# A softplus series on GpSimd in place of VectorE, in the state space layer of a hybrid block

## The chip, the cores and the metric

The kernel runs on one core of a Trainium2 chip. A core has five engines that matter here, each with its own queue, which it works off in order: TensorE (PE, with its weight loads shown as PEld), VectorE (DVE), ScalarE (ACT), GpSimd (POOL) and SyncE (SP), which only issues transfers. The metric is the device time of one execution in microseconds, the median of three runs.

## The reference, cut to what matters

The block is four residual layers over 2 sequences of 1024 tokens with width 512: a state space layer, a mixture of experts, an attention layer, and the mixture again. Only the first one is touched. In it, all values float32:

```
xBCzA  = norm(x) @ in_proj.T                 # 2048 channels, 1024 gates z, 64 heads A_log
xBC    = silu(causal_conv4(xBCzA[:2048]) + bias)
dt     = softplus(A_log)                     # per token and head: 64 numbers a token
y      = chunked_scan(x, -dt, B, C, 128)     # decays are exp of sums of -dt in a chunk
y      = (y + D * x / dt) * silu(z + z_bias)
x     += y @ out_proj.T
```

The kernel makes softplus as max(a, 0) + log1p(exp(-|a|)), and the logarithm by a series: with y = exp(-|a|) and s = y / (y + 2), it is s times a polynomial of degree 8 in s squared, with the nine numbers of `ATANH`.

## The kernel before, in words

**Tiling.** A segment is 256 tokens, two chunks of 128, so there are 8 segments and 16 chunks. `segment_inputs` makes all that a segment needs. It is a generator: each `yield` is a step after which the caller may put in other work. Its first step makes the norm and the transposed tokens. Its second, which is called the head here, is the one that changes: `ps_dt` (L570) is A_log by 16 matmul records, `al` (L579) brings it to SBUF as a tile of 128x128 (128 tokens, two chunks of 64 heads), `sp_y` (L581) is -|a|, ScalarE takes its exponential in place (L582), and then come the instructions of the series: L584 (y + 2), L585 (reciprocal), L587 (s), L589 (s squared), L591 (first coefficient), L593 seven times, L594, and L596, which writes `dt`. After it come `dw` = D / dt (L599, L600). The third step has TensorE sum `dt` with three triangular or full matrices (`ps_cum`, L607), ScalarE takes the decays (`decay`, L609), VectorE copies the sums (`cum`, L612), and TensorE makes the same sums as rows (`ps_row`, L615), which go to DRAM (`sums`, L621) to be read back broadcast.

The 24 steps after it make the channels: `ps_ch` (L638) is 128 channels of the projection, in one of three buffers in PSUM that it shares with the gates' `ps_z` (L663). VectorE does the convolution, a first tap (L641) and three further ones (L645), and so frees the buffer; ScalarE takes the silu of four such tiles (L649).

**The chunks.** `own` takes one chunk: eight times it loads a tile `m` of 128x1024 (L802), GpSimd subtracts `cum` (L806), ScalarE makes two passes (L808, L809), VectorE multiplies by the masked scores (L810), and TensorE multiplies with x into `ps_y` (L814). VectorE multiplies by the gates (`yT`, L833) and TensorE projects out (`ps_out`, L840). `prologue` starts the next chunk: GpSimd makes `xd` and `y` (L718, L720), VectorE `yo` (L735), GpSimd adds it (L741) and scales the state (L764).

**Order.** The inputs of segment n+1 are traced beside the chunks of segment n: 27 steps over two chunks. The order of one engine's instructions isn't written out. The framework orders them once, when the kernel is built, by the order of tracing and its own estimate of when each operand is there, and sets the semaphores. On the chip each engine keeps to that order. So VectorE's queue holds series and convolution in turn, though the text emits the series in one piece.

**Buffers.** `al`, `sp_y`, `sp_r`, `sp_s2` have one buffer each, used once per segment. `dt`, `dw`, `decay` have two, `m` six.

Of the kernel before, what the change touches and what calls it, by code (L numbers as in the profile page):

```python
# [14 lines left out]
ALU = mybir.AluOpType  # L15
# [28 lines left out]
ATANH = [2.0 / (2 * k + 1) for k in range(9)]  # L44
# [45 lines left out]
def hybrid_layer_kernel(ctx: ExitStack, tc: tile.TileContext, a: dict, out: bass.AP):  # L90
    nc = tc.nc
# [426 lines left out]
    with ExitStack() as sa:  # L518
# [34 lines left out]
        def segment_inputs(b, s, before):  # L553
# [24 lines left out]
            al = sp.tile([P, n], F32, tag="al", name="al", bufs=1)  # L578
            nc.vector.tensor_copy(al, ps_dt.rearrange("p c h -> p (c h)"))  # L579
            y = sp.tile([P, n], F32, tag="sp_y", name="sp_y", bufs=1)  # L580
            nc.vector.scalar_tensor_tensor(y, al, -1.0, al, ALU.mult, ALU.min)  # L581
            nc.scalar.activation(y, y, AF.Exp)  # L582
            r = sp.tile([P, n], F32, tag="sp_r", name="sp_r", bufs=1)
            nc.vector.tensor_scalar(r, y, 2.0, None, ALU.add)  # L584
            nc.vector.reciprocal(r, r)  # L585
            sv = y
            nc.vector.tensor_mul(sv, y, r)  # L587
            s2 = sp.tile([P, n], F32, tag="sp_s2", name="sp_s2", bufs=1)
            nc.vector.tensor_mul(s2, sv, sv)  # L589
            acc = r  # L590
            nc.vector.tensor_scalar(acc, s2, ATANH[-1], None, ALU.mult)  # L591
            for c in ATANH[-2:0:-1]:
                nc.vector.scalar_tensor_tensor(acc, acc, c, s2, ALU.add, ALU.mult)  # L593
            nc.vector.scalar_tensor_tensor(acc, acc, ATANH[0], sv, ALU.add, ALU.mult)  # L594
            dt = sp.tile([P, CPS, NH], F32, tag="dt", name="dt")
            nc.vector.scalar_tensor_tensor(dt.rearrange("p c h -> p (c h)"), al, 0.0, acc, ALU.max, ALU.add)  # L596

            dw = sp.tile([P, CPS, NH], F32, tag="dw", name="dw")
            nc.vector.reciprocal(dw, dt)  # L599
# [258 lines left out]
        def inputs(n):  # L858
            b, s, _ = place_of(n * CPS)
            segs[n] = yield from segment_inputs(b, s, segs[n - 1][0] if s else None)  # L860
# [328 lines left out]
```

## Time and profile before

| what | value |
|---|---|
| runs | 2338.01 us median (2336.97 to 2341.95) |
| profiled execution | 2334.98 us, of which the span from first to last instruction is 2333.3 us |
| state space layer, 0 to 790 us of the span | PE 742.3 us busy, DVE 585.6, ACT 485.3, POOL 384.8 |
| the rest, 790 to 2333 us | PE 1488.8 us busy, DVE 828.9, ACT 371.0, POOL 655.5 |
| the eight heads begin (L579) at | 17.7, 73.3, 158.8, 255.8, 349.8, 439.4, 536.5, 636.7 us |
| L584 to L596 without L585, VectorE, all heads | 104 instructions, 46.3 us busy (4.7 + 4.9 + 7.4 + 6.2 + 18.7 + 2.2 + 2.2) |

A group's line gives line, engine, operation, tile written and tiles read, shapes, count, then busy time in us and the mean of one in ns, then the engine's idle time before it. A line of the timeline gives start and length in us, and in brackets how long the engine was idle before and what it waited for. A line of the waits gives the total in us, how often, and the longest.

### The profile page before, as it was taken

What the parts mean: (1) busy time and instruction counts of PE and PEld (TensorE: products, weight loads), DVE (VectorE), ACT (ScalarE), POOL (GpSimd) and SP (SyncE); (2) the same over time, 40 slices, a digit from 0 to 9 for tenths busy, and PEclk for the clock granted to TensorE, in tenths of its full rate; (3) what the DMA queues carried; (4) which work ended last, traced back from release to release, by engine and by line L of the source; (5) the groups of instructions that cost most, each with busy time, mean ns of one, the idle gap of its engine ahead of it and who ended that gap; (6) DMA issues with size and microseconds to landing.
All of it is one profiled execution on the core that took longest, in us unless ns stands there. A gap on an engine that the chain in (4) does not pass through costs nothing.

```text
span 2333.3 us, 29887 instructions
## 1 busy us (share of the span) xinstructions
PE 2231.1 (96%) x11018; PEld 1442.1 (62%) x11018; DVE 1414.5 (61%) x2115; ACT 856.3 (37%) x1414; POOL 1040.3 (45%) x695
## 2 busy tenths in 40 slices
PE   9999999999999999999789999999899999999998
PEld 7776677676776566555455656555566665565554
DVE  7777877777676630000339999884499999720002
ACT  4656576666566422221122332222223332212221
POOL 3544464455645300001457777642678776210002
PEclk9999999999999999999899999999999999999999
DMA  8444454454554477876355564433466554368766
GB/s 282 148 145 146 162 183 155 138 196 138 178 174 178 161 264 260 301 261 239 111 189 182 178 224 171 149 117 129 177 222 215 200 206 138 122 239 298 294 244 196
DMA packets 116369, 449.67 MB, mean 193 GB/s; under 512 B 15104, under 2 KB 17920, under 8 KB 103808
## 3 DMA queue, kind: packets, MB, share of 16 engines
q1 hardware_dynamic: 88960, 380.28, 46.9%
q0 software_dynamic: 12480, 40.90, 5.7%
q10 hardware_dynamic: 14784, 26.58, 3.0%
q8 instruction: 88, 1.44, 0.2%
q14 instruction: 57, 0.47, 0.1%
HBM read 402.09 MB, written 45.61 MB: 192 GB/s over the span
## 4 chain that ended last, share of the span: by engine, by line
PE 64%; DVE 13%; POOL 8%; DMA 6%; ACT 5%; issue 5%; SPq 0%; POOLq 0%; ACTq 0%; DVEq 0%
PE ps_o L476 13%; PE ps_g L445 12%; PE ps_u L454 11%; PE ps_ch L638 5%; PE ps_out L840 5%; POOL pr L1007 3%; PE ps_z L663 3%; DMA m<-sums 3%; DVE sc L1011 3%; PE ps_xnT L187 2%; PE ps_y L814 2%; DVE pv L1027 2%; DVE o L1028 2%; POOL m L806 2%; PE ps_hT L466 2%
## 5 line engine op out<-in xcount | busy, mean ns | idle before, releaser
L1007 POOL TENSOR_TENSOR pr<-qk 128x1536 f32<-128x1536 f32 x128 | 441.4, 3458 | 145.3 <-DVE sc L1011 71.0
L806 POOL TENSOR_TENSOR m<-m,cum 128x1024 f32<-128x1024 f32 x128 | 243.5, 1911 | 318.3 <-DMA m<-sums 221.5
L455 DVE TENSOR_TENSOR h<-h,ps_u 128x352 f32<-128x352 f32 x156 | 80.4, 515 | 479.8 <-PE ps_u L454 473.9
L380 POOL DMA_INDIRECT xg<-normed,r_tok x92 | 90.1, 979 | 539.3 <-PE ps_xnT L187 465.4
L638 PE MATMUL ps_ch<-xnT,w_ch 128*128 128x259 f32 x1024 | 260.1, 400 | 17.4 <-DVE chan L645 14.5
L476 PE MATMUL ps_o<-w_d,hT 128*128 128x512 f32 x552 | 254.5, 596 | 6.9 <-issue 3.7
L447 ACT ACTIVATE h<-ps_g 128x352 f32<-128x352 f32 x156 | 72.4, 464 | 494.7 <-PE ps_g L445 485.5
L1011 DVE TENSOR_REDUCE sc<-pr 128x32 f32<-128x1536 f32 x128 | 224.2, 1752 | 38.3 <-POOL pr L1007 38.2
L445 PE MATMUL ps_g<-w_gu,xT 128*128 128x352 f32 x736 | 237.0, 462 | 2.6 <-ACT hT L468 1.2
L454 PE MATMUL ps_u<-w_gu,xT 128*128 128x352 f32 x736 | 236.7, 461 | 0.0
L638 PEld LDWEIGHTS ps_ch<-xnT,w_ch 128*128 128x128 f32 x1024 | 192.6, 195 | 65.6 <-issue 34.4
L808 ACT ACTIVATE m<-m 128x1024 f32<-128x1024 f32 x128 | 134.4, 1053 | 184.9 <-POOL m L806 184.8
L476 PE MATMUL ps_o<-s_d,hT 128*128 128x512 f32 (+1 forms) x384 | 183.7, 611 | 12.6 <-ACT hT L468 10.3
L445 PEld LDWEIGHTS ps_g<-w_gu,xT 128*128 128x128 f32 x736 | 137.0, 190 | 91.0 <-issue 32.2
L482 ACT COPY y<-ps_o 128x512 f32<-128x512 f32 x92 | 53.9, 586 | 372.3 <-PE ps_o L476 372.2
L645 DVE SCALAR_TENSOR_TENSOR chan<-ps_ch,convw,chan 128x256 f32<-128x256 f32 x384 | 180.9, 476 | 7.4
L476 PEld LDWEIGHTS ps_o<-w_d,hT 128*128 128x128 f32 x552 | 104.9, 192 | 114.9 <-issue 92.3
L454 PEld LDWEIGHTS ps_u<-w_gu,xT 128*128 128x128 f32 x736 | 133.5, 191 | 63.0 <-issue 7.1
L445 PE MATMUL ps_g<-s_gu,xT 128*128 128x352 f32 x512 | 170.7, 469 | 1.4 <-ACT h L447 1.4
L454 PE MATMUL ps_u<-s_gu,xT 128*128 128x352 f32 x512 | 168.0, 466 | 0.0
L810 DVE TENSOR_TENSOR m<-m,g 128x1024 f32<-128x1024 f32 x128 | 150.6, 1211 | 20.0 <-ACT m L809 19.8
L1027 DVE TENSOR_TENSOR pv<-sc,vT 128x1024 f32<-128x1024 f32 x128 | 155.8, 1217 | 1.1
(209 smaller groups left out, 3470.5 us busy)
## 6 DMA issues: line engine op xcount, KB each, us to landing
w_gu<-in_wall SPq DMA_DIRECT2D x92, 1408.0 KB, 7.9
w_d<-in_wall SPq DMA_DIRECT2D x92, 768.0 KB, 4.5
m<-sums SPq DMA_DIRECT2D x128, 512.0 KB, 4.6
w_ch<-in_wch SPq DMA_DIRECT2D x96, 512.0 KB, 3.9
made<-y ACTq DMA_DIRECT2D x92, 256.0 KB, 7.9
xT<-columns SPq DMA_DIRECT2D x64, 256.0 KB, 4.7
normed<-xn SPq DMA_DIRECT2D x32, 256.0 KB, 2.1
columns<-p_xnT SPq DMA_DIRECT2D x32, 256.0 KB, 3.2
```

The lines of the kernel that those rows point to most:

```text
L445: nc.tensor.matmul(ps_g, xT[:, k, :], both[:, k, 0, :], start=(k == 0), stop=(k == KD - 1))
L454: nc.tensor.matmul(ps_u, xT[:, k, :], both[:, k, 1, :], start=(k == 0), stop=(k == KD - 1))
L476: nc.tensor.matmul(ps_o, hT[:hn, c, :], wd[:hn, c, :], start=(c == 0), stop=(c == len(HC) - 1))
L638: nc.tensor.matmul(ps, w[:, ct % 2, k], xnT[:, k, :], start=(k == 0), stop=(k == KD - 1))
L645: nc.vector.scalar_tensor_tensor(c[:, i], ps[:, tap : tap + SEG], convw[:, ct, tap : tap + 1], c[:, i], ALU.mult, ALU.add)
L806: nc.gpsimd.tensor_tensor(m, m, bc(cum[:, j, h0 : h0 + 8], 2, P), ALU.subtract)
L808: nc.scalar.activation(m, m, AF.Relu)
L810: nc.vector.tensor_tensor(m, m, bc(gs[e][:, i, :], 1, 8), ALU.mult)
L840: nc.tensor.matmul(ps_out, yT[:, e, i, :], w_out[:, 2 * i + e, :], start=(e == 0 and i == 0), stop=(e == 1 and i == 3),)
L1007: nc.gpsimd.tensor_mul(pr, bc(qks[t][:, 0, i : i + IC, :], 2, AH), bc(qks[t][:, 1], 1, IC))
L1011: nc.vector.tensor_reduce(scores[t][:, i : i + IC, :], products.pop((t, i)), AX.X, ALU.add)
L1027: nc.vector.tensor_tensor(pv, bc(scores[t][:, i : i + IC, :], 2, DH), bc(vs[t], 1, IC), ALU.mult)
```

## The change

The sums and products of the series go from VectorE to GpSimd. The reciprocal (L585) stays on VectorE between the first and the second of them, as do `al` and `sp_y` ahead of the series and `dw` behind it. Each instruction of the form (in + constant) x in, one on VectorE, becomes two: a sum with a constant and a product. `al` is clamped in place.

```diff
             nc.scalar.activation(y, y, AF.Exp)
             r = sp.tile([P, n], F32, tag="sp_r", name="sp_r", bufs=1)
-            nc.vector.tensor_scalar(r, y, 2.0, None, ALU.add)
+            nc.gpsimd.tensor_scalar(r, y, 2.0, None, ALU.add)
             nc.vector.reciprocal(r, r)
             sv = y
-            nc.vector.tensor_mul(sv, y, r)
+            nc.gpsimd.tensor_mul(sv, y, r)
             s2 = sp.tile([P, n], F32, tag="sp_s2", name="sp_s2", bufs=1)
-            nc.vector.tensor_mul(s2, sv, sv)
+            nc.gpsimd.tensor_mul(s2, sv, sv)
             acc = r
-            nc.vector.tensor_scalar(acc, s2, ATANH[-1], None, ALU.mult)
+            nc.gpsimd.tensor_scalar(acc, s2, ATANH[-1], None, ALU.mult)
             for c in ATANH[-2:0:-1]:
-                nc.vector.scalar_tensor_tensor(acc, acc, c, s2, ALU.add, ALU.mult)
-            nc.vector.scalar_tensor_tensor(acc, acc, ATANH[0], sv, ALU.add, ALU.mult)
+                nc.gpsimd.tensor_scalar(acc, acc, c, None, ALU.add)
+                nc.gpsimd.tensor_mul(acc, acc, s2)
+            nc.gpsimd.tensor_scalar(acc, acc, ATANH[0], None, ALU.add)
+            nc.gpsimd.tensor_mul(acc, acc, sv)
             dt = sp.tile([P, CPS, NH], F32, tag="dt", name="dt")
-            nc.vector.scalar_tensor_tensor(dt.rearrange("p c h -> p (c h)"), al, 0.0, acc, ALU.max, ALU.add)
+            nc.gpsimd.tensor_scalar(al, al, 0.0, None, ALU.max)
+            nc.gpsimd.tensor_add(dt.rearrange("p c h -> p (c h)"), al, acc)
```

## The prediction

> **What bounds the kernel now.** I read the page's busy times first, then the same for the state space layer alone, then TensorE's waits in it.
>
> ```profile
> span 2333.3 us, 29887 instructions
> ...
> PE 2231.1 (96%) x11018; PEld 1442.1 (62%) x11018; DVE 1414.5 (61%) x2115; ACT 856.3 (37%) x1414; POOL 1040.3 (45%) x695
> ```
>
> ```profile
> 0.00:790.00 790.00, 742.34 (x5405) 545.93 (x5406) 585.62 (x1043) 485.26 (x556) 384.77 (x287) 0.97 0.51 170
> 790.00:2333.00 1543.00, 1488.76 (x5614) 896.13 (x5614) 828.88 (x1073) 370.99 (x858) 655.52 (x408) 0.99 0.58 204
> ```
>
> TensorE bounds the program. In the layer that changes it is idle for 790 - 742 = 48 us; nothing behind 790 us is touched. A change to another engine can only give back a part of those 48 us, or add to them. So the question is which of these 48 us VectorE causes at the heads.
>
> ```profile
> PE ps_ch L638 <- DVE chan L645: 14.5, 7, 3.7
> ...
> PE ps_s L750 <- DVE yo L735: 3.2, 1, 3.2
> ...
> PE ps_cum L607 <- DVE dt L596: 0.2, 1, 0.2
> ```
>
> The largest cause is TensorE waiting for a projection buffer that the convolution frees. The same view cut to the heads puts all of it there: by head 2.2, 0.8, 3.7, 1.7, 1.5, 2.9, 2.7 and 0.2 us (with waits of `ps_z` on the same convolution), 15.7 us in all. The wait for `dt` itself is 0.2 us. The timeline of the third head shows how it comes about (the first line's wait is for the exponential):
>
> ```profile
> 163.24 0.33 DVE L584 TENSOR_SCALAR sp_r<-sp_y 128x128 f32<-128x128 f32 x1 [1.52 <-ACT sp_y L582]
> 163.44 3.81 POOL L806 TENSOR_TENSOR m<-m,cum 128x1024 f32<-128x1024 f32 x2
> ...
> 164.48 0.45 DVE L641 TENSOR_SCALAR chan<-ps_ch,convw,convb 128x256 f32<-128x256 f32 x1
> ...
> 165.81 1.58 DVE L589 TENSOR_TENSOR sp_s<-sp_y 128x128 f32<-128x128 f32 x1
> ...
> 168.32 0.47 DVE L645 SCALAR_TENSOR_TENSOR chan<-ps_ch,convw,chan 128x256 f32<-128x256 f32 x1
> ...
> 168.93 2.63 PE L638 MATMUL ps_ch<-xnT,w_ch 128*128 128x259 f32 x8 [3.65 <-DVE chan L645]
> ...
> 174.18 0.27 DVE L596 SCALAR_TENSOR_TENSOR dt<-al,sp_r 128x128 f32<-128x128 f32 x1
> ```
>
> TensorE has filled its three buffers and stands at 165.28. The first convolution, four instructions that need about 1.65 us (0.45 and three of 0.40 from start to start), takes from 164.48 to 168.79, because a series instruction lies between any two of them, and those are stretched: 1.58 us for L589, which takes 0.27 elsewhere. They are stretched just while GpSimd works on `m`. The convolution itself is not.
>
> **What the change takes from VectorE.** Thirteen instructions a head: 46.3 us over eight heads. Undisturbed they would be 2 x 0.21 + 11 x 0.275 = 3.4 us a head, 28 us in all, so 19 us are stretch. What counts is when the first convolution ends. Third head: GpSimd's additions to `y` end at 163.44, the new first sum takes 0.3, the reciprocal follows 0.1 later and takes 0.95, the convolution starts near 164.7 and ends near 166.4, so TensorE waits 1.1 in place of 3.65: 2.5 gained. Fourth: start 260.3, end 262.0, and TensorE runs out only at 263.74: all 1.7 gained. Fifth, sixth, seventh: likewise ended 0.5 to 1.2 us before TensorE runs out: 1.5, 2.9, 2.7. First head: the convolution follows the reciprocal closely already, ending 21.7 in place of 22.0: 0.4. Second and eighth: 0.8 and 0.2. Sum 12.7 us. Not all arrives: the chain that ended last is TensorE for 64% of the span, and behind a removed wait the next one can open (the loads of `m`, ScalarE's passes). I take 64%: **-8.1 us**.
>
> **What it adds to GpSimd.** Twenty-two instructions a head, 11 with one tensor and a constant, 11 with two tensors. The trace of before has neither at 128x128, so from the nearest rows:
>
> ```profile
> L741 POOL TENSOR_TENSOR y<-y,yo 128x512 f32<-128x512 f32 x28 | 35.7, 1290 | 0.6
> ...
> L159 POOL TENSOR_SCALAR rstd<-mv 128x1 f32<-128x1 f32 x48 | 11.7, 245 | 68.8 <-ACT xn L175 36.6 <-DVE mv L156 21.8 <-DVE xn L181 7.8
> ...
> L113 POOL TENSOR_SCALAR_AFFINE_SELECT upper<-ones 128x128 f32<-128x128 f32 x1 | 0.3, 290 | 0.0
> ```
>
> One tensor: between 0.245 (one element) and, say, 0.36; I take 0.29, the row of the same size. Two tensors: L741 is 1.27 us at 512 elements; with some 0.13 us fixed, as the smallest rows have, that is 2.2 ns an element, so 0.41 at 128, bounds 0.33 and 0.50. L159 to L160, a dependent pair, leaves 0.075 between end and start. So 11 x 0.365 + 11 x 0.485 = 9.4 us a head, 7.7 of it busy; busy time of POOL goes from 1040 to about 1102 us. The rule of the Trainium skill ("GPSIMD Engine Reference", Engine selection) is about twice VectorE's time for two inputs: 2 x 0.275 = 0.55, and a head of 10.9 us; I keep the row's 0.41 and the rule as the far end.
>
> The cover for it is GpSimd's idle time behind each head:
>
> ```profile
> 167.21 2.23 POOL L764 TENSOR_TENSOR state<-state,decay 64x512 f32<-64x512 f32 x2
> 191.32 1.90 POOL L806 TENSOR_TENSOR m<-m,cum 128x1024 f32<-128x1024 f32 x1 [21.88 <-PE ps_y L814]
> ```
>
> 22 us here, and 8.9 to 22.6 at the later heads. What is queued behind the series on GpSimd is the two `m` and two `state` multiplies; put behind it, the last `m` would leave GpSimd near 176 and ScalarE near 178, where VectorE takes it up at 178.4 now. So that costs nothing, but with no more than a us to spare; without this cover it is up to 2 us a head.
>
> **A rule against the change.** "Perfetto Trace Analysis" (Optimizing Scalar/DVE Operations) warns that GpSimd and VectorE share an SBUF read port, so that moving work between the two may not help. The stretched L589 and L581 are that, in this trace. By the rule the convolution beside the series would be held for up to 7.7 us a head, and the gain would be gone (+60 us at most). But the instructions that stay read one operand from PSUM:
>
> ```profile
> L645 DVE SCALAR_TENSOR_TENSOR chan<-ps_ch,convw,chan x384: 373/482/486, 20.4 to 719.9; 128x256 f32<-128x256 f32 x192
> ...
> L810 DVE TENSOR_TENSOR m<-m,g x128: 1200/1210/1222, 67.0 to 789.8; 128x1024 f32<-128x1024 f32 x128
> ```
>
> 384 and 128 of them, with and without GpSimd beside them, and the longest is within 2% of the median. I take zero.
>
> **Where a new wait can come.** `dt` is not needed for its own sake before the next segment, some 80 us on. But TensorE has `ps_cum`, VectorE L599 and L600, and ScalarE `decay` in their queues at fixed places; if `dt` is late there, all behind them stands: projections, convolutions, silu. Before, from the exponential's end to `dt` took 8.4 us in the first head and 10 to 13 in the others. After: 0.54 for the first sum, 1.05 for the reciprocal and its hop, 9.0 for the rest: 10.6 us, if nothing lies between. With the two `m` and two `state` multiplies in the gaps (3.8 + 2.2) it is 16.6. TensorE comes to `ps_cum` at 175.3 now, and 2.5 us sooner after the change; `dt` would be there at 173.9 to 179.9. With the old order that is a stall of 1 to 7 us; but the order is made anew, and whoever plans it sees the longer series and puts projections and gates ahead of `ps_cum`. The stall is then only the error of the plan: bounds 0 and 7 us a head. In this layer TensorE waits once for anything that GpSimd makes (`xd`, 1.0 us), and `dt` cost 0.2 us once; I take 0.25 us a head, **+2.0 us**.
>
> **Sum.** -8.1 + 2.0 = -6.1 us, on the profiled 2334.98 us (2333.3 span and 1.7 around it). The median of the runs lies 3.0 us above that execution, and I take the same difference from it: 2338.0 - 6.1 = 2332.
>
> **Rivals.** (1) Faster, as worked out, 2324 to 2333: 42%. (2) The gain is hidden: TensorE's waits at the heads go, but as many us open elsewhere, at loads of `m`, at ScalarE's reloaded tables (1.28 us each) or at `dt`; within 0.2% (4.7 us, about what can be told from no change), near 2337: 23%. For it: VectorE, GpSimd and ScalarE follow each other closely in this layer. Against it: TensorE is busy for 94% of it. (3) Slower: `dt` comes late to `ps_cum`. The place is TensorE's queue, and VectorE's at L599. The price is the lateness s times eight; it eats the gain at s = 8.1 / 8 = 1.0 us and decides for slower by over 0.2% at 1.6 us. That is 0.07 us for each of 22 instructions that the plan has too short, or one `m` of 1.9 us put ahead of the series' next step without being counted. At 2.5 us it is +20 - 8 = +12 us, 2350. For it: in the later layers ScalarE waits 101 us, 27 times, for a chain of three small GpSimd instructions (`shift`, L167) that stands in GpSimd's queue among long ones. Against it: GpSimd is idle right behind the heads. 35%. That the change doesn't do what it says is hardly possible: the instructions change engine whatever the order.
>
> **How the numbers follow.** Likeliest 2332. The range leaves about 1 in 10 on either side: below, all 15.7 us of waits gone and no stall, 2322; above, s near 3.2 us, 8 x 3.2 - 8 = +18, 2356. Chances: 0.42 faster, 0.23 same, 0.35 slower.
>
> **What would show it.** Right: `ps_ch` waits for `chan` under 5 us in place of 14.5; POOL near 1100 us busy and 104 fewer VectorE instructions; the rows of the series at 0.29 and 0.41 us; convolutions without gaps at the heads. Wrong: a wait of TensorE or VectorE for `dt` of more than 1 us a head; L645 or L810 stretched; an `m` of GpSimd late to L810; projections held by a reciprocal (L585) that waits for GpSimd's first sum behind an `m`.

## The result: 4.0% slower

The changed kernel takes 2433.72 us (median of five runs, 2427.74 to 2435.78) against 2338.01 us. The ratio is 1.0399, with a 95% interval from 1.0385 to 1.0414. The forecast was 2332 us with a range up to 2356. Below, line numbers of the changed kernel are four higher than before from the head on (`ps_cum` is L611, `dt` L600, `chan` L645 and L649, `ps_ch` L642).

The top of the changed kernel's page, the span and the busy times:

```profile
span 2434.1 us, 29917 instructions
...
PE 2256.8 (93%) x11018; PEld 1461.3 (60%) x11018; DVE 1381.2 (57%) x2011; ACT 839.5 (34%) x1400; POOL 1124.6 (46%) x871
```

VectorE has 104 instructions fewer and GpSimd 176 more, as the change says. GpSimd is busy 84.3 us longer, where 62 were forecast. TensorE has the same 11018 records, and they took 25.7 us longer. To see where, both spans are cut where the state space layer ends. The columns are the stretch, then its length, the busy time and count of PE, PEld, DVE, ACT and POOL, then TensorE's granted clock, the DMA share and GB/s. Before:

```profile
0.00:804.70 804.70, 757.04 (x5490) 555.04 (x5494) 592.20 (x1057) 487.03 (x559) 385.82 (x290) 0.97 0.51 168
804.70:2333.30 1528.60, 1474.06 (x5532) 887.02 (x5528) 822.29 (x1059) 369.23 (x855) 654.48 (x405) 0.99 0.59 206
```

After:

```profile
0.00:893.50 893.50, 776.82 (x5490) 570.32 (x5494) 555.00 (x953) 470.53 (x545) 470.25 (x466) 0.92 0.45 152
893.50:2434.10 1540.60, 1479.94 (x5532) 890.95 (x5528) 826.15 (x1059) 368.97 (x855) 654.37 (x405) 0.98 0.58 204
```

The layer is 88.8 us longer and the rest 12.0, together the 100.8 us by which the two profiled executions differ. In the layer TensorE is idle for 893.5 - 776.8 = 116.7 us in place of 804.7 - 757.0 = 47.7, which is 69.0 more. It is busy 19.8 us longer for the same 5490 records, at a granted clock of 0.92 in place of 0.97.

The waits of the changed kernel in this layer (total in us, how often, longest), those of the engines in question:

```profile
PE ps_cum L611 <- POOL dt L600: 69.3, 8, 12.6
PE ps_ch L642 <- DVE chan L649: 17.8, 7, 4.1
```

```profile
DVE dw L603 <- POOL dt L600: 74.8, 8, 11.9
...
DVE sp_r L586 <- POOL sp_r L585: 22.5, 8, 5.4
```

TensorE's new idle time has one name: eight times, once a head, it stands at `ps_cum` for `dt`, 6.1 to 12.6 us each. The wait for the convolution, which was to shrink from 14.5 to under 5 us, is 17.8. VectorE stands at the same `dt`, and now also at the reciprocal for GpSimd's first sum. The third head, the one that the prediction worked through, in the timeline of the changed kernel:

```profile
180.00 0.29 ACT L582 ACTIVATE sp_y<-sp_y 128x128 f32<-128x128 f32 x1
180.53 1.90 POOL L810 TENSOR_TENSOR m<-m,cum 128x1024 f32<-128x1024 f32 x1
182.40 0.53 POOL L599 TENSOR_SCALAR al<-al 128x128 f32<-128x128 f32 x1
182.90 0.54 POOL L585 TENSOR_SCALAR sp_r<-sp_y 128x128 f32<-128x128 f32 x1
183.40 1.90 POOL L810 TENSOR_TENSOR m<-m,cum 128x1024 f32<-128x1024 f32 x1
183.47 0.95 DVE L586 RECIPROCAL sp_r<-sp_r 128x128 f32<-128x128 f32 x1 [4.67 <-POOL sp_r L585]
...
185.26 1.05 POOL L768 TENSOR_TENSOR state<-state,decay 64x512 f32<-64x512 f32 x1
...
186.27 0.45 POOL L588 TENSOR_TENSOR sp_y<-sp_y,sp_r 128x128 f32<-128x128 f32 x1
186.81 3.56 PE L642 MATMUL ps_ch<-xnT,w_ch 128*128 128x259 f32 x8 [3.81 <-DVE chan L649]
...
198.27 0.45 POOL L600 TENSOR_TENSOR dt<-al,sp_r 128x128 f32<-128x128 f32 x1
198.75 0.95 DVE L603 RECIPROCAL dw<-dt 128x128 f32<-128x128 f32 x1 [9.94 <-POOL dt L600]
198.77 0.80 PE L611 MATMUL ps_cum<-dt,upper 128*128 128x128 f32 x2 [8.39 <-POOL dt L600]
...
201.40 2.07 PE L787 MATMUL g<-chan 64*128 64x128 f32 x14
```

The exponential ends at 180.3. GpSimd first does an `m` and the clamp of `al`, so the first sum starts 2.6 us later. The reciprocal is done at 184.4, but the next product waits behind an `m` and a `state` multiply until 186.27. From there the series needs 12.45 us, a second `state` multiply in it. Together 18.4 us from exponential to `dt`. TensorE is at `ps_cum` 10.1 us after the exponential and stands there until `dt` comes. Meanwhile nothing runs on TensorE, and VectorE stands too, at `dw`.

The same place before, TensorE alone:

```profile
168.93 2.63 PE L638 MATMUL ps_ch<-xnT,w_ch 128*128 128x259 f32 x8 [3.65 <-DVE chan L645]
171.50 2.07 PE L783 MATMUL g<-chan 64*128 64x128 f32 x14
173.50 2.00 PE L663 MATMUL ps_z<-xnT,w_ch 128*128 128x256 f32 x8
175.34 0.38 PE L607 MATMUL ps_cum<-dt,upper 128*128 128x128 f32 x2
```

Before, `ps_cum` came behind the scores `g` and the first of two gate tiles, 4 us of work. After, it comes directly behind `ps_ch`, and `g` and both gate tiles are behind it. The new order asks for `dt` earlier, although `dt` comes later. The timelines of the other heads agree: TensorE reaches `ps_cum` 7.2 to 12.2 us behind the exponential, where it took 9.2 to 13.3 before, and in each of the eight heads it comes earlier than it did; `dt` is done after 13.8 to 19.9 us, where it took 8.4 to 13.0.

### The profile page after: what moved, and what is told of

Read it like the earlier page. It is cut to its first block, busy times and chain, and to the rows that moved or that the text cites. A ratio compares the mean times of both kernels' runs of the same rounds, so it can differ in the third digit from the quotient of the medians.

```text
span 2434.1 us, 29917 instructions
## 1 busy us (share of the span) xinstructions
PE 2256.8 (93%) x11018; PEld 1461.3 (60%) x11018; DVE 1381.2 (57%) x2011; ACT 839.5 (34%) x1400; POOL 1124.6 (46%) x871
## 4 chain that ended last, share of the span: by engine, by line
PE 62%; POOL 12%; DVE 9%; DMA 7%; issue 5%; ACT 4%; SPq 0%; POOLq 0%; ACTq 0%; DVEq 0%
PE ps_o L476 13%; PE ps_g L445 11%; PE ps_u L454 11%; PE ps_out L844 5%; PE ps_ch L642 4%; DMA m<-sums 3%; PE ps_z L667 3%; POOL pr L1011 3%; POOL m L810 3%; DVE sc L1015 2%; PE ps_xnT L187 2%; PE ps_y L818 2%; PE ps_ao L1047 2%; DVE o L1032 2%; DVE pv L1031 2%
## 5 line engine op out<-in xcount | busy, mean ns | idle before, releaser
L642 PE MATMUL ps_ch<-xnT,w_ch 128*128 128x259 f32 x1024 | 261.8, 403 | 19.8 <-DVE chan L649 17.8
L642 PEld LDWEIGHTS ps_ch<-xnT,w_ch 128*128 128x128 f32 x1024 | 193.2, 196 | 68.8 <-issue 37.5
L476 PE MATMUL ps_o<-s_d,hT 128*128 128x512 f32 (+1 forms) x384 | 186.2, 618 | 15.8 <-ACT hT L468 10.2
L812 ACT ACTIVATE m<-m 128x1024 f32<-128x1024 f32 x128 | 134.5, 1053 | 185.2 <-POOL m L810 185.1
L649 DVE SCALAR_TENSOR_TENSOR chan<-ps_ch,convw,chan 128x256 f32<-128x256 f32 x384 | 180.2, 478 | 8.7
```

The source lines that it names most:

```text
L476: nc.tensor.matmul(ps_o, hT[:hn, c, :], wd[:hn, c, :], start=(c == 0), stop=(c == len(HC) - 1))
L642: nc.tensor.matmul(ps, w[:, ct % 2, k], xnT[:, k, :], start=(k == 0), stop=(k == KD - 1))
L649: nc.vector.scalar_tensor_tensor(c[:, i], ps[:, tap : tap + SEG], convw[:, ct, tap : tap + 1], c[:, i], ALU.mult, ALU.add)
L812: nc.scalar.activation(m, m, AF.Relu)
```

## The experiments

The theory, A in the expectations: the time is lost because the readers of `dt` hold fixed places in the queues of TensorE and VectorE, and the chain on GpSimd reaches `dt` after these engines have reached those places. The rivals: GpSimd's time itself costs (B: its other work comes late, or the shared port holds VectorE up), the sums and decays made from `dt` are needed sooner than thought (C), or TensorE's clock costs, which falls behind each wait. Ratios are to runs of the kernel before that were taken beside them on the same chip; its median there was between 2342 and 2346 us.

### The readers of `dt` moved back

`dw`, `ps_cum`, `decay`, `cum`, `ps_row` and `sums` are issued behind the second group of four channel tiles and its gates, held there by an order on the last gate matmul and the last convolution tap. First on the changed kernel, then on the kernel before, with the series on VectorE.

```diff
-            dw = sp.tile([P, CPS, NH], F32, tag="dw", name="dw")
...
             for n, quad in enumerate((2, 3, 0, 1)):
                 yield from channels(quad)
                 yield from gates(n)
+                if n == 1:
+                    with tc.issue_after(last["mm"].ins), tc.issue_after(last["tap"].ins):
+                        dw = sp.tile([P, CPS, NH], F32, tag="dw", name="dw")
...
+                        ps_cum = pp.tile([P, 3, CPS, NH], F32, tag="misc", name="ps_cum")
...
```

> The changed kernel, with the instructions that read dt (dw, ps_cum, decay, cum, ps_row, sums) traced and held behind the second quad of channels and its gates, some 22 us of TensorE's work later; the series stays on GpSimd. Theory A (TensorE and VectorE stand at the place where dt's readers lie in their queues): the wait of ps_cum for dt falls from 69 us to under 5 us, the granted clock goes back to about 0.98, and the time is 2325 to 2345 us. Theory B (GpSimd's 84 us of added work hold VectorE at the shared port or delay m): GpSimd works as before, so the time stays above 2400 us. Theory C (the sums and decays are needed sooner than thought): the time stays above 2400 us, with waits moved to the consumers of cum and decay.

> The kernel before, series on VectorE, with the same instructions held behind the second quad: what moving them does by itself. Theory A: dt is there long before, so within 0.3% of before, 2331 to 2345 us; with e1 the difference is what the series costs or gains when nobody stands at dt, by the record 0 to 13 us in e1's favour. Theories B and C: B expects about before too; C expects it slower, by 20 us or more.

Measured: the changed kernel with its readers moved takes 2362.57 us, ratio 1.0078 [1.0055, 1.0100]. The kernel before with the same move takes 2367.27, ratio 1.0079 [1.0048, 1.0110]. The layer of the changed kernel so moved, and two of its waits:

```profile
0.00:819.70 819.70, 761.62 (x5490) 561.07 (x5494) 560.88 (x953) 453.29 (x533) 470.63 (x466) 0.96 0.50 165
```

```profile
DVE sp_r L586 <- POOL sp_r L585: 24.2, 8, 6.6
...
PE ps_ch L617 <- DVE chan L624: 17.8, 7, 5.4
```

There is no wait for `dt` left on any engine, and the loss falls from 4.0 to 0.8%: the layer is 73.8 us shorter than in the changed kernel, 58.6 of it TensorE's idle time and 15.2 its busy time. So A is shown for most of the loss: the series is as long as it was, on the same engine, and only its readers' places differ. Both runs missed A's ranges, though. The first is above its 2325 to 2345 us, and the second is not within 0.3% of before: the move by itself costs 0.8%, with the series where it always was. The second trace has 8.2 us more idle and 9.2 us more busy time in the layer than the kernel before, and the waits of `ps_b` and `ps_x` for ScalarE are 6.1 us longer; why, wasn't followed further. It is also 19.6 us longer behind the layer, where nothing was changed, so it is open how much of the 0.8% the layer makes:

```profile
822.10:2370.30 1548.20, 1485.26 (x5532) 894.33 (x5532) 826.22 (x1059) 369.20 (x855) 654.55 (x405) 0.98 0.58 203
```

With both so placed, series on GpSimd and series on VectorE take the same time.

### How far back, and whose queue

The same with the readers behind the first group (`n == 0`), and, on the other side, with `dw` left right behind the series while the rest stays behind the second group.

```diff
-                if n == 1:
+                if n == 0:
```

> As e1, but held behind the first quad and its gates only, some 11 us of TensorE's work in place of 22. Theory A: dt is still late in most heads; the wait of ps_cum is about half of 69 us, 20 to 45 us, and the time lies between, 2360 to 2400 us. Theories B and C: as the changed kernel, above 2400 us.

```diff
             nc.gpsimd.tensor_add(dt.rearrange("p c h -> p (c h)"), al, acc)
+            dw = sp.tile([P, CPS, NH], F32, tag="dw", name="dw")
+            nc.vector.reciprocal(dw, dt)
+            nc.vector.tensor_mul(dw, dw, bc(dskip, 1, CPS))
...
                 if n == 1:
...
-                        dw = sp.tile([P, CPS, NH], F32, tag="dw", name="dw")
-                        nc.vector.reciprocal(dw, dt)
-                        nc.vector.tensor_mul(dw, dw, bc(dskip, 1, CPS))
```

> As e1 for TensorE (ps_cum and what follows held behind the second quad), but dw stays directly behind the series, so that VectorE's queue alone still has a reader of dt at its old place. Theory A: VectorE stands at the reciprocal of dt for about as long as in the changed kernel (75 us there), the convolutions behind it come late, and TensorE waits for them at ps_ch instead: ps_ch waits of 40 to 80 us, time 2370 to 2430 us. A variant of A in which TensorE's own place is all that counts: 2325 to 2350 us.

Measured: 2383.30 us, ratio 1.0156 [1.0135, 1.0177], and 2400.09 us, ratio 1.0234 [1.0216, 1.0251]. Waits of the first:

```profile
DVE dw L655 <- POOL dt L600: 38.8, 8, 8.5
...
PE ps_row L668 <- DVE x L853: 18.7, 5, 5.3
```

and of the second:

```profile
DVE dw L602 <- POOL dt L600: 73.1, 8, 11.9
...
PE ps_ch L621 <- DVE chan L628: 25.8, 10, 4.7
...
PE ps_out L845 <- DVE yT L838: 18.2, 4, 4.8
```

Halfway back, half of VectorE's wait is left. TensorE's wait at `ps_cum` is down to 2.2 us, where A expected 20 to 45, but a part of it comes back under another name, behind VectorE; the time is in A's range. In the second kernel TensorE waits for `dt` nowhere. Yet VectorE alone, standing at `dw` for 73.1 us, costs 1.6% more than with `dw` moved (1.0234 to 1.0078): the convolutions and `yT` queued behind it come late to TensorE. The time is in A's range again, and the waits are spread more widely than A said: 25.8 us at `ps_ch`, 11.7 at `ps_z` for the same convolutions and 18.2 at `ps_out`, where 40 to 80 were expected at `ps_ch` alone. Either queue passes the lateness on.

### GpSimd's time without the lateness

The kernel before, its series on VectorE as it was, with a copy of GpSimd's 22 instructions issued behind `dt` on the same tiles. Nobody reads what the copy makes.

```diff
+            nc.gpsimd.tensor_scalar(r, al, 2.0, None, ALU.add)
+            nc.gpsimd.tensor_mul(sv, al, r)
...
+            nc.gpsimd.tensor_scalar(al, al, 0.0, None, ALU.max)
+            nc.gpsimd.tensor_add(s2, al, r)
             dw = sp.tile([P, CPS, NH], F32, tag="dw", name="dw")
```

> The kernel before, series on VectorE, and behind it at each head a copy of the whole GpSimd series of 22 instructions on the same tiles, whose result nobody reads. Theory A: nobody waits for it, so within 0.4% of before, 2329 to 2348 us, although GpSimd is busy about 84 us longer. Theory B: slower by most of what the change cost, 2390 us or more. Theory C: as A.

Measured over nine runs: 2352.30 us, ratio 1.0023 [1.0005, 1.0042]. The page's busy times of this kernel:

```profile
PE 2234.3 (95%) x11018; PEld 1445.4 (62%) x11018; DVE 1413.7 (60%) x2115; ACT 856.1 (36%) x1414; POOL 1127.2 (48%) x871
```

GpSimd is as busy as in the changed kernel (1127 and 1125 us), and it costs 0.2% where the change cost 4.0, within the 0.4% that A expected. So GpSimd's time is nearly free, as the prediction had it, and neither its other work nor the port carries the loss. One limit: the copy can start only when VectorE has written `dt`, so it runs some us later than the series does. That the series at its own place doesn't hold GpSimd's other work up is seen in the changed kernel itself, where ScalarE waits for `m` in this layer as long as before (185.1 and 184.8 us).

### The first sum back on VectorE

The reciprocal's operand is made on VectorE again; the other 21 instructions stay on GpSimd. Once with the readers at their old places, once with the readers moved behind the second group.

```diff
-            nc.gpsimd.tensor_scalar(r, y, 2.0, None, ALU.add)
+            nc.vector.tensor_scalar(r, y, 2.0, None, ALU.add)
```

> The changed kernel with only the first sum (y + 2) back on VectorE; dt's readers at their own places. Theory A: VectorE no longer waits 22 us for GpSimd's first sum and TensorE waits less for the convolutions (under 10 us in place of 17.8), but it reaches ps_cum the sooner and stands there for dt; dt itself comes about half a microsecond a head sooner. So 2405 to 2435 us, far from before. If the wait at the first sum were the main cost: 2370 us or less.

> As e1, and the first sum (y + 2) back on VectorE, so that the reciprocal there doesn't wait for GpSimd. Theory A: VectorE's wait for GpSimd's first sum, 22 us in the changed kernel, goes, and TensorE's wait for the convolutions at the heads falls from about 18 us to under 8: 3 to 12 us faster than e1. If the reciprocal's wait costs nothing: the same as e1 within 0.2%.

Measured, readers at their old places: 2422.66 us, ratio 1.0346 [1.0326, 1.0365]. Readers moved: 2332.75 us, ratio 0.9949 [0.9925, 0.9973]. Waits of the first:

```profile
DVE dw L603 <- POOL dt L600: 82.5, 8, 13.5
PE ps_cum L611 <- POOL dt L600: 77.7, 8, 12.9
...
PE ps_ch L642 <- DVE chan L649: 8.3, 3, 5.7
```

The convolution's wait falls by 9.5 us (17.8 to 8.3), and `ps_cum`'s grows by 8.4 (69.3 to 77.7): TensorE only arrives sooner at the place where it stands for `dt`. So of what the first sum costs, 0.5% shows (1.0399 to 1.0346). With nobody standing at `dt` it is 1.3% (1.0078 to 0.9949). The layer of the second kernel, its wait for the convolution, and its third head:

```profile
0.00:798.80 798.80, 750.38 (x5490) 554.09 (x5494) 566.97 (x961) 453.09 (x533) 467.52 (x458) 0.97 0.51 169
```

```profile
PE ps_ch L617 <- DVE chan L624: 9.1, 4, 5.9
```

```profile
167.68 0.95 DVE L586 RECIPROCAL sp_r<-sp_r 128x128 f32<-128x128 f32 x1
168.55 0.45 DVE L620 TENSOR_SCALAR chan<-ps_ch,convw,convb 128x256 f32<-128x256 f32 x1
169.04 1.00 DVE L624 SCALAR_TENSOR_TENSOR chan<-ps_ch,convw,chan 128x256 f32<-128x256 f32 x2
...
171.03 1.99 PE L617 MATMUL ps_ch<-xnT,w_ch 128*128 128x259 f32 x8 [1.52 <-DVE chan L624]
...
184.95 0.46 POOL L600 TENSOR_TENSOR dt<-al,sp_r 128x128 f32<-128x128 f32 x1
...
198.42 0.94 DVE L655 RECIPROCAL dw<-dt 128x128 f32<-128x128 f32 x1
```

This version is faster than both kernels, and by more than the 3 to 12 us over the first that A expected: between the two traces the layer is 20.9 us shorter, 9.7 of it idle time (8.7 at `ps_ch`) and 11.2 busy time. Here is what the change could give: the convolutions follow each other without series instructions between, and TensorE waits 1.52 us where it waited 3.65 before. `dt` is done 18.1 us after the first sum, no sooner than in the changed kernel (15.8), but its first reader on VectorE comes 13 us after it. Against the kernel before with the same move, the gain of the series, all but its first sum, on GpSimd is 1.3% (1.0079 to 0.9949; each is a ratio to runs of before on its own chip).

### The clock behind the waits

To see whether TensorE's slower clock is a cost of its own, `ps_cum` was held behind the first four projections (`dw` right behind the series), and TensorE was given 60, 30 or no transposes of `s2` ahead of it, whose result nobody reads.

```diff
+                        for _ in range(FILL):
+                            nc.tensor.transpose(ps_cum[:, 3].rearrange("p c h -> p (c h)"), s2, ident)
```

> The changed kernel, with ps_cum held behind the first quad's four projections (nearly its own place), and 60 transposes of a tile of the series, whose result nobody reads, on TensorE ahead of it: TensorE works while it would stand. Beside it e5b without the transposes. Theory A with the clock (standing lowers the granted clock of what follows): e5 is 10 to 25 us faster than e5b although TensorE has 480 instructions more, and its granted clock in the first 890 us is 0.95 or above in place of about 0.92. Theory A without the clock (TensorE's longer busy time has another cause): e5 is equal to e5b or slower.

> The changed kernel with ps_cum held behind the first quad's four projections, dw at its own place, without transposes: the changed kernel's order but for one or two projections. All theories: within 1% of the changed kernel, 2410 to 2458 us, with about 60 to 75 us of waits of ps_cum for dt.

> As e5 with 30 transposes a head in place of 60, some 3.6 us, which is less than any of the eight waits for dt, so that they lie within them. If standing lowers the clock of what follows: ps_cum's records behind the transposes at 0.4 to 0.5 us for two, as before the change, in place of 0.8, and the time 2405 to 2424 us, under e5b's 2426. If e5's 29 us over e5b come from the transposes' place in the order and not from their length: 2440 us or more here too.

Measured: 2455.06 us, ratio 1.0490 [1.0452, 1.0528] with 60; 2425.62 us, 1.0367 [1.0340, 1.0394] with 30; 2426.35 us, 1.0342 [1.0317, 1.0368] with none. The theory with the clock had expected 60 to be 10 to 25 us faster than none, and 30 to be below 2424 us; neither came. TensorE's waits at 60:

```profile
PE ps_out L848 <- ACT row L672: 18.9, 6, 4.4
PE ps_ch L622 <- DVE chan L629: 18.7, 7, 4.6
PE ps_cum L662 <- POOL dt L601: 14.4, 6, 4.5
```

This does not settle it. The 60 transposes (55.8 us) fill the wait from 67.2 to 14.4 us, and the matmuls behind them run at full speed again: `ps_cum`'s second matrix takes 275 ns in the median in place of 421. But the layer's idle time falls by 26.7 us only (116.0 to 89.3), since the order changed with them and `ps_out` now waits 18.9 us for ScalarE; the kernel is slower. With 30, a wait of about 5 us a head stands behind the transposes, the median is 421 ns still, and the intervals of with and without overlap. TensorE's busy time without the transposes themselves is 772.7 us with 60 (828.5 - 55.8), 768.6 with 30 (797.5 - 28.9) and 774.5 with none. So filling the waits gave back only 2 to 6 us of busy time. The traces record when the granted clock changes, and these records say why that tells little: the clock is 1.00 or 0.50 in them, and the part of TensorE's busy time that lies at 0.50 hardly changed, 90.9 us with 60, 86.9 with 30 and 92.3 with none. With 60 there still are stands at `ps_cum` and new ones at `ps_out`. The runs didn't take the slow clock away; what it costs is read from the traces below.

## Why the prediction was wrong, step by step

**What bounds the kernel, and the 48 us.** Right: the loss in the layer is TensorE standing (69.0 us) and busy for longer (19.8).

**The gain from VectorE (12.7 us of waits, 8.1 of them in time).** The mechanism is right, and the version with moved readers and the first sum on VectorE shows it: third head 3.65 to 1.52 us, where 1.1 was forecast. In the changed kernel itself it did not come. The step let the first sum follow the additions to `y` at once. In fact an `m` and the clamp stand ahead of it in GpSimd's queue, 2.6 us in this head, and VectorE stood 22.5 us in all at a reciprocal with the convolutions behind it. That was on the list of signs that it is wrong, but had no price in the sum. It measured +3.3 us at `ps_ch` in place of -8.1.

**The cost on GpSimd.** Two rows of the series in the changed kernel:

```profile
L594 POOL TENSOR_SCALAR sp_r<-sp_r 128x128 f32<-128x128 f32 x56 | 29.6, 529 | 4.8
...
L595 POOL TENSOR_TENSOR sp_r<-sp_r,sp_s 128x128 f32<-128x128 f32 x56 | 25.4, 454 | 4.4
```

The product is 0.454 us, within its bounds of 0.33 and 0.50 and near the 0.41 taken. The sum with a constant is 0.529, where 0.29 was taken and 0.36 was the upper bound. The row taken for it, a mask of the same size, was of another operation; the same operation at one element (0.245) and the slope that the prediction drew from L741 (2.2 ns an element, 0.28 for 127 more) would have given 0.52. From start to start the two are 0.54 and 0.61 us, so 22 are 12.7 us a head and not 9.4. The rule of the Trainium skill ("GPSIMD Engine Reference", Engine selection) has it the other way round: twice VectorE's time with two inputs, and about line rate, so no such factor, with one. Here two inputs cost 1.65 times VectorE's 0.275 us, and one input 2.5 times its 0.21 (VectorE's times are those of instructions that nothing stretched); the measurement decides.

**The cover, and the shared port.** Right. The copy that nobody reads costs 0.2%. The instructions that read PSUM are not stretched in the changed kernel (shortest, median and longest in ns):

```profile
L649 DVE SCALAR_TENSOR_TENSOR chan<-ps_ch,convw,chan x384: 384/483/486, 21.6 to 809.1; 128x256 f32<-128x256 f32 x192
...
L814 DVE TENSOR_TENSOR m<-m,g x128: 1202/1214/1223, 77.6 to 878.6; 128x1024 f32<-128x1024 f32 x128
```

**The new wait, 0.25 us a head.** This is the step that failed. It took 69.3 / 8 = 8.7 us. The working had both ends of it: `dt` 10.6 to 16.6 us behind the exponential, TensorE at `ps_cum` some 12 us behind it less the gain of 2.5, a stall of 1 to 7 us with the old order. The shape of this sum was right. The series is 12.7 us a head and not 9.4; with these 3.3 us more its bounds for `dt` are 13.9 to 19.9, and the eight heads measured 13.8 to 19.9. Its stall with the old order would then have been 4 to 10 us, and the eight were 6.1 to 12.6. The choice of 0.25 rested on one sentence, that the plan sees the longer series and puts projections and gates ahead of `ps_cum`. It did the reverse: in the third head the scores and the gate tiles went behind `ps_cum`, and in all eight heads TensorE came there earlier than before. That its estimate of these GpSimd instructions is far below 0.5 us each would explain this; it is argued from the order and not shown. The single wait of 1.0 us for `xd`, taken as a measure of the plan's error, was for another instruction at another place, and said nothing of this one.

**The clock, a term that was missing.** Behind each stand TensorE runs slower. The second matrix of `ps_cum` before and after (ns), and the 12 us behind the third head's wait:

```profile
L607 PE MATMUL ps_cum<-dt,below x16: 275/275/275, 28.1 to 652.0; 128*128 128x128 f32 x16
```

```profile
L611 PE MATMUL ps_cum<-dt,below x16: 421/422/423, 33.3 to 736.7; 128*128 128x128 f32 x16
```

```profile
199.00:211.00 12.00, 12.00 (x38) 7.00 (x39) 9.32 (x15) 3.20 (x4) 0.00 (x0) 0.66 0.02 5
```

The same from the end of the wait to where the clock is full again:

```profile
198.77:207.00 8.23, 8.23 (x29) 5.38 (x30) 6.47 (x13) 2.41 (x4) 0.00 (x0) 0.50 0.03 8
```

The granted clock over the 12 us is 0.66 in this head and 0.66 to 0.86 behind the eight waits. In six of the eight it fell to 0.50 some 2.0 to 5.3 us after TensorE stopped, in the other two it was there already; once TensorE works again it stays there for 3.5 to 8.3 us, 44 us in all. The Trainium skill ("TensorE: Matmul & The Clock Gate", Part 1) says that about 3.4 us of idle time halve the clock, and as much busy time frees it. All eight waits are longer than that, so by this page one would have estimated 8 x 3.4 x 1/2 = 14 us beside the stalls; 19.8 us of longer busy time is what the layer shows. The halving agrees with the traces; the time until the clock is free again was here between that figure and more than twice it.

Counted over the whole layer from the same clock records, TensorE works at half clock for 95.0 us in the changed kernel and 45.7 before, 49.3 us more. A matmul that takes 421 ns in place of 275 loses 35% of that time, and one that follows the clock fully loses half. This estimate from the traces makes 17 to 25 us, and the 19.8 lie within it, at 0.40 for each us. With that one factor the other runs fit as well: the layer's busy time, without the transposes, is 750 to 777 us in the twelve traces, and less 0.40 of its part at half clock it is 734 to 740 in all of them. So the longer busy time is the clock's, to within a few us. On the whole it rises with the idle time, though not in proportion (idle / busy in the layer, us): 48.4 / 750.4 in the fastest version, 47.7 / 757.0 before, 58.1 / 761.6 and 55.9 / 766.2 with the readers moved, 89.9 / 776.7 with all but `dw` moved, 116.7 / 776.8 in the changed kernel. Which stand brings which slow stretch was followed only for the eight waits.

**The sum with the measured terms.** +69.1 at `ps_cum` (69.3 less the 0.2 of before), +3.3 at `ps_ch`, -3.4 for the other idle time of the layer, +19.8 busy, +12.0 behind the layer: 100.8 us. Even the step's own upper end, 7 us a head, would have given 8 x 7 - 8.1 = +48, half of this. The 12 us behind the layer (half of them busy time, at a clock of 0.98 in place of 0.99) have no cause in the change that these runs show. In the traces of the ten experiments the same lines of the kernel take 1531.4 to 1548.2 us there, so the changed kernel's 1540.6 lies among them, and the 1528.6 of before is the shortest of all: a part of the 100.8 us may be no more than the spread between executions.

**The rivals and the range.** The third rival was the case: the place, TensorE's queue and VectorE's at `dw`, and the sign as it said. Its price was put at 2.5 us a head in the example, and the range stopped at 3.2, though the working allowed 7. An argument on what a planner would do was allowed to narrow a bound that came from the trace.

## What to carry to other kernels

When a step moves to a slower engine, compare its latency, not its busy time, with the moment at which each reader's engine reaches that reader in its queue: here some 85 us of GpSimd's time cost 0.2%, and its lateness in front of two queues cost most of 4.0%. Move the readers back first and then the work, measure what that move costs alone (0.8% here), and keep on the old engine whatever a waiting engine needs at once (the first sum alone decided between 0.8% slower and 0.5% faster). Don't count on the order to adapt: look in the new trace at whether the reader went back or forward.

## What was not expected of the hardware

On GpSimd a sum of a 128x128 tile with a constant (0.529 us) takes longer than a product of two such tiles (0.454), while on VectorE it is the shorter one (0.21 and 0.275). Behind a stand of TensorE of 6 to 13 us, matmuls of 275 ns take 421, and the granted clock stays at half for 3.5 to 8.3 us of work.
